# A two-layer graph network on one core: inner Strassen products a step apart, and p1 copied into p2's bank

## The chip, the cores and the metric

The kernel runs on one core of a Trainium2 chip. Its time is device time in microseconds (us) of one execution of the whole program, here the median of three. TensorE (PE) multiplies into PSUM[...]; VectorE (DVE) and ScalarE (ACT) read and write PSUM and SBUF; GpSimd (POOL) works on SBUF only; SyncE (SP) issues the DMAs.

## What is computed

The input x has 16 batches of 1024 nodes with 512 features; adj is one 1024 x 1024 matrix. All values are float32.

```python
# layer 0
h = maximum(layernorm(x), 0)
x = x + (adj @ h[b]) @ weight + bias
# layer 1
u = maximum(layernorm(x), 0)
g = u @ W
s1, s2 = g @ a[:512], g @ a[512:]
e = leaky_relu(s1[:, None] + s2[None, :], 0.2) * adj
x = x + elu(softmax(e, axis=1) @ g + beta * g)
```

## The kernel before

**Products.** Each large product is a 2 x 2 block product by Winograd's form of Strassen: seven products p1 to p7 in place of eight (`PRODUCTS`, line 44). A product takes a left block or block sum (A11, A12, A22, S1 to S4) and a right one (B11, B21, B22, T1 to T4) and adds into one of three pairs of PSUM banks, Y, W or X. Y holds p1, then p1+p6, then +p7, then +p4; X holds p5, then +p3; W holds p2 alone. T1 = B12 - B11, T2 = B22 - T1, T3 = B22 - B12 and T4 = B21 - T2. After each half of a product (`p` or `q`, 0 and 1), `ReadA` (line 121) takes the bank out: ACT copies p1, p6, p5 and p4 to SBUF, DVE adds p2, p7 and p3 to what is there and forms the sums that the next product needs.

**Two layers, two parts each.** A batch of a layer has a first part (layer 0: adj times h, names `y_`; layer 1: the softmax's transpose times u, names `z_`) and a second (times the weights, class `Weighted`, line 322, names `po_` and `pq_`). All 16 batches of layer 0 run first, then all of layer 1.

**The inner level of layer 0.** From batch 1 on, six of the seven products of the first part (all but p7) are themselves seven-product forms on half-size blocks (`inner_steps`, line 206). An inner product has steps in the order r1, r4, r5, r6, r2, r7, r3, two matmuls of 256 columns each (on PE four instructions, 0.86 us). r1 writes a bank of its own, y; ACT copies it out; r5 writes x, which ACT copies out, then r6 and r7 add to y. Step r5's left operand is the first of the sums that `inner_left` (line 405) makes on DVE. After r7 DVE adds the inner sums into the first half of the product's bank, after r3 into the second half. Products run in pairs with their steps alternating: (p1, p2), then (p5, p6), seven turns each; then p3's steps beside p7's plain matmuls; then p4's beside the first product of the second part (lines 279 to 320). Before, p7's first matmul follows p3's first step.

**The order of everything else.** Every engine's instructions stay in the order in which they are written (`InOrder`, line 103). A plan, a dictionary from step number to calls, says what runs after which step: `after(k)`, where k counts the 14 product halves of a part, or in layer 0's inner form 28 turns. The plan of layer 0 (`plan_out`, line 1081) puts beside the products the statistics (`stats`, on ACT), normalisation (`relu`, on ACT, after three small POOL instructions) and logits (`logits`, on DVE) of the batch before, and `inner_left` for p5, p6, p3 and p4 at steps 0, 1, 13 and 18.

**The softmax of layer 1.** While batch b is multiplied, the softmax of batch b+1 is made (`SOFTMAX_A`, line 1144, and `SOFTMAX_B`). `M0` to `M7` make the masked logits of eight chunks (ACT, then DVE with a mask from DRAM), `L2` to `L7` load masks on SP, `X` and `x` send the maxima through DRAM, `N` and `n` read them on DVE, `E0` to `E7` are the exponentials on ACT, each followed at once by its two 32 x 32 transposes on DVE (`exp`, line 795); `S`, `s`, `D` and `d` handle the sums. `LATE_A` (line 1150) forms T3 and T4 of the batch that is being multiplied, in halves a and b: T4a after step 9, T4b after step 11.

**The second part of layer 1** (`layer1_b`, line 867). Of its products p1, p6 and p5 are copied by ACT to SBUF (`part`), p2, p7 and p3 are added to that by DVE (`rest`), and then `elu` takes the result through two activations on ACT and two additions; p4 goes to `elu` straight from PSUM.

The few lines that set the order of layer 1's first part:

```python
    SOFTMAX_A = {
        -1: "M0 L2", 0: "M1 L3", 1: "M2 L4", 2: "M3 L5 X", 3: "M4 L6", 4: "M5 L7", 5: "N B E0",
        6: "M6", 7: "E1 M7 x", 8: "E2", 9: "E3 S", 10: "n b E4", 11: "E5", 12: "E6", 13: "E7 s",
    }
    LATE_A = {5: "T3a", 6: "T3b", 9: "T4a", 11: "T4b"}
```

## Time and profile before

| | |
|---|---|
| median of three runs | 2464.78 us (2459.21 to 2466.63) |
| profiled execution | 2472.3 us, its span 2470.5 us |
| layer 0, from the first product to layer 1's first | up to 1169.15 us |
| a batch of layer 0, as batch 4 | 305.60 to 377.24 us |
| a batch of layer 1, as batch 1 | 1248.85 to 1329.48 us |
| DVE, ACT, POOL busy | 1909.7, 1542.7, 546.2 us |

Most instructions are recorded through helpers and so stand on one line (L111); they are told apart by the names of their tiles: `y_` and `po_` for layer 0, `z_` and `pq_` for layer 1, then the bank (`z_Y`), SBUF blocks (`z_C`, `z_S`), `pT` for the transposed exponentials and their sums T, `in_p` for inner sums, `e` for logits. In a timeline a line has the start, the time, the engine, the operation, out<-in, the number of instructions merged, and in brackets the idle time before it with what ended it. A waits line has the engine and tile that waited, what it waited for, the total in us, the number of times and the longest. A line of stretches has each engine's busy time and instructions, then the granted share of PE's clock, the DMA share and GB/s.

### The profile page before, as it was taken

Reading aid. Unit: us, or ns where it says so; the run is one execution under the profiler, and the core shown is the slowest. Engines: PE = TensorE matmul, PEld = TensorE weight load, DVE = VectorE, ACT = ScalarE, POOL = GpSimd, SP = SyncE. Lnnn points to the kernel's source line nnn. Section 1 sums busy time; section 2 is a strip of 40 time slices with the busy share of each in tenths; the row PEclk is TensorE's granted clock in tenths of the full one; section 3 lists DMA queues with packets and bytes.
Section 4 is the critical chain, followed back from the end, with each engine's and each line's share of the span. In section 5 each row is a group of like instructions: output and inputs, shape, how many; then the busy total and the mean of one; then the engine's idle time right before and its main releaser. Section 6 shows DMA issues by size and latency. Waiting matters only on the chain.

```text
span 2470.5 us, 29533 instructions
## 1 busy us (share of the span) xinstructions
PE 2324.3 (94%) x8344; PEld 1604.4 (65%) x8344; DVE 1909.7 (77%) x4165; ACT 1542.7 (62%) x4115; POOL 546.2 (22%) x680
## 2 busy tenths in 40 slices
PE   9999999999999999999999898988998899999998
PEld 5787777788777777886446544654465546554555
DVE  7777778878877878778787778777877778777864
ACT  3766666676666767664566656665676567556643
POOL 1333221323323222221022202220222012211220
PEclk9999999999999999999999999999999999999999
DMA  6433434433343343325443454445443443344431
GB/s 200 137 128 129 137 121 138 154 120 128 129 145 120 129 154 129 115 99 186 154 147 122 138 165 151 131 131 169 159 128 126 161 155 123 106 141 155 146 97 34
DMA packets 194292, 336.02 MB, mean 136 GB/s; under 512 B 78800, under 2 KB 86992, under 8 KB 194128
## 3 DMA queue, kind: packets, MB, share of 16 engines
q1 hardware_dynamic: 193808, 333.61, 40.9%
q8 instruction: 66, 1.08, 0.2%
q14 instruction: 98, 0.80, 0.1%
q10 hardware_dynamic: 320, 0.52, 0.1%
HBM read 228.33 MB, written 109.91 MB: 137 GB/s over the span
## 4 chain that ended last, share of the span: by engine, by line
PE 27%; DVE 12%; ACT 7%; DMA 5%; SPq 2%; issue 2%; POOL 1%; DVEq 0%; ACTq 0%; POOLq 0%
PE z_Y L111 9%; PE pq_Y L111 8%; ACT e L111 4%; DVE e L111 3%; PE pq_X L111 3%; DMA md<-mx 2%; PE pq_W L111 2%; PE z_X L111 2%; DVE pT L111 2%; PE z_W L111 2%; SPq L111 2%; DVE z_C L111 2%; DMA mask<-maskd 1%; DVE z_S L111 1%; DVE pT_T L111 1%
## 5 line engine op out<-in xcount | busy, mean ns | idle before, releaser
L111 POOL TENSOR_TENSOR x<-x,r 128x512 f32<-128x512 f32 x120 | 209.9, 1762 | 984.9 <-DVE x L111 592.3
L111 ACT ACTIVATE e<-e,nm 128x256 f32<-128x256 f32 x480 | 237.2, 498 | 121.8 <-DVE nm L111 121.8
L111 DVE CUSTOM_DVE_ANT_0 e<-e,mask 128x256 f32<-128x256 f32 x512 | 244.0, 530 | 33.6 <-DMA mask<-maskd 18.1
L111 PE MATMUL z_Y<-pT_T,ul_U 128*128 128x512 f32 x256 | 153.5, 755 | 94.3 <-DVE pT_T L111 94.3
L111 DVE STREAM_TRANSPOSE pT<-e 128x512 f32<-128x512 f32 x240 | 156.3, 689 | 108.3 <-ACT e L111 108.2
L111 PE MATMUL z_Y<-pT,ul_U 128*128 128x512 f32 x512 | 225.2, 592 | 0.0
L111 ACT ACTIVATE e<-s2b,s1b 128x256 f32<-128x256 f32 x512 | 215.0, 504 | 8.7 <-PE po_Y L111 8.7
L111 ACT COPY z_C<-z_Y 128x512 f32<-128x512 f32 x96 | 56.2, 586 | 254.2 <-PE z_Y L111 245.7
L111 POOL TENSOR_TENSOR xr<-xr,bias_bc 128x512 f32<-128x512 f32 x128 | 161.9, 1287 | 222.4 <-DVE xr L111 190.0
L111 PE MATMUL y_Y<-adjT_B,h 128*128 128x512 f32 (+1 forms) x332 | 166.3, 607 | 38.6 <-ACT y_C L111 36.7
L111 PE MATMUL po_Y<-w_c,y_C 128*128 128x256 f32 x768 | 188.3, 379 | 0.0
L111 PEld LDWEIGHTS z_Y<-pT_T,ul_U 128*128 128x128 f32 x256 | 61.5, 248 | 183.6 <-DVE pT_T L111 107.5
L111 DVE CUSTOM_DVE_ANT_0 junk<-xr,v_bc 128x512 f32<-128x512 f32 x240 | 166.4, 693 | 11.1
L111 PE MATMUL pq_Y<-w_c,z_C 128*128 128x256 f32 x768 | 173.7, 379 | 0.0
L111 PEld LDWEIGHTS z_Y<-pT,ul_U 128*128 128x128 f32 x512 | 97.0, 190 | 116.2 <-issue 107.9
L111 PEld LDWEIGHTS pq_Y<-w_c,z_C 128*128 128x128 f32 x768 | 145.8, 190 | 27.1 <-issue 7.7
L111 PEld LDWEIGHTS po_Y<-w_c,y_C 128*128 128x128 f32 x768 | 145.9, 190 | 20.3 <-issue 0.5
L111 ACT ACTIVATE r<-z,rs 128x256 f32<-128x256 f32 x192 | 95.8, 499 | 81.1 <-DVE z L111 81.1
L111 ACT ACTIVATE h<-x,nb_h,r_h 128x512 f32<-128x512 f32 (+1 forms) x132 | 98.2, 793 | 50.2 <-POOL nb_h L111 50.2
L111 ACT ACTIVATE junk<-xr 128x512 f32<-128x512 f32 x120 | 75.9, 632 | 72.6 <-DVE xr L111 70.0
L111 PE MATMUL po_X<-w_c,y_S 128*128 128x256 f32 x512 | 115.7, 379 | 0.0
L111 PE MATMUL pq_X<-w_c,z_S 128*128 128x256 f32 x512 | 115.6, 379 | 0.0
(224 smaller groups left out, 5229.4 us busy)
## 6 DMA issues: line engine op xcount, KB each, us to landing
mask<-maskd SPq DMA_DIRECT2D x128, 512.0 KB
x<-in_x_dram SPq DMA_DIRECT2D x64, 512.0 KB
xr<-in_x_dram SPq DMA_DIRECT2D x256, 128.0 KB
x1d<-xr SPq DMA_DIRECT2D x64, 512.0 KB
ul_U<-ud_U SPq DMA_DIRECT2D x64, 512.0 KB
x<-x1d SPq DMA_DIRECT2D x64, 512.0 KB
out_dram<-x SPq DMA_DIRECT2D x252, 128.0 KB
ud_U<-xr SPq DMA_DIRECT2D x60, 512.0 KB
```

The costliest lines, as they stand in the source:

```text
L111: return lambda *args, **kwargs: tc.keep_in_program_order(f(*args, **kwargs))
```

## The change

In layer 0's inner form the second pair is (p6, p5), and within both pairs the two products are one step apart: the first product's first two steps, then one step of each in turn, then the second's last two. p6's halves are read out after turns 4 and 5, p5's after turn 6. Steps r4 and r5 change places in products that add to a bank already in use (p6, p3, p4). p3's first two steps come before p7's first two matmuls. `inner_left` for p6 and p5 change places; that for p3 stays at step 13.

In layer 1, both parts, ACT copies p1 into p2's bank W, p2 is added to it there without the start flag, and the result is copied out once (first part) or goes straight to `elu` (second part); the second part runs p5 before p2, except in the last batch. The transposes become steps `V0` to `V7` of their own, mostly one step after their exponentials; `M0` moves from step -1 to step 0, and T4b from step 11 to step 10.

```diff
-NODES_LAST = tuple(PRODUCTS[k] for k in (0, 1, 2, 3, 5, 4, 6))
+FORKED = tuple((*p[:4], p[4] and p[0] != "p2", p[5]) for p in PRODUCTS)
+NODES_LAST = tuple(FORKED[k] for k in (0, 1, 2, 3, 5, 4, 6))
+P5_EARLY = tuple(FORKED[k] for k in (0, 3, 1, 2, 4, 5, 6))
...
             if prod == "p1":
+                act.copy(self.fork(p) if self.fork else self.block("C11", p), ps)
+            elif prod == "p2" and self.fork:
                 act.copy(self.block("C11", p), ps)
...
+        def fork(p):
+            banks["W", p] = bank(f"{name}_W{p}")
+            return banks["W", p]
...
-            return [partial(step, r) for r in ("r1", "r4", "r5", "r6", "r2", "r7", "r3")]
+            order = ("r1", "r4", "r5") if first else ("r1", "r5", "r4")
+            return [partial(step, r) for r in (*order, "r6", "r2", "r7", "r3")]
...
-        for pair in (("p1", "p2"), ("p5", "p6")):
-            turns = list(zip(*(inner_steps(prod) for prod in pair)))
-            for m, turn in enumerate(turns):
-                for step in turn:
-                    step()
+        for one, two in (("p1", "p2"), ("p6", "p5")):
+            ones, twos = inner_steps(one), inner_steps(two)
+            turns = ones[0:2] + [t for m in range(5) for t in (twos[m], ones[m + 2])] + twos[5:]
+            for m in range(7):
+                turns[2 * m]()
+                turns[2 * m + 1]()
                 if m == 0 and k:
                     reads("p2", 0)
                     reads("p2", 1)
-                elif m > 4:
-                    for prod in pair:
-                        if prod != "p2":
-                            reads(prod, m - 5)
+                elif m in (4, 5):
+                    reads(one, m - 4)
+                elif m == 6 and k:
+                    reads(two, 0)
+                    reads(two, 1)
                 after(k + m)
...
-        for m in range(7):
-            inn[m]()
-            pla[m if m < 4 else m + 1]()
+        turns = [(inn[0], inn[1]), pla[0:2], (inn[2], pla[2]), (inn[3], pla[3]), (inn[4], pla[4])]
+        turns += [(inn[5], pla[5]), (inn[6], *pla[6:8])]
...
+        def fork(self, kind, q, ps):
+            b = self.banks[kind, q] = bank(f"{self.name}_{kind}{q}")
+            act.copy(b.rearrange("p (i o) -> p i o", i=2), ps)
...
             if prod == "p1":
-                part(0, 0, q, ps)
-            elif prod == "p2":
-                rest(0, 0, q, ps, 2 + q)
+                weighted1[0].fork("W", q, ps)
...
-                elu(1, 0, q, ps, 12 + q)
+                elu(0 if prod == "p2" else 1, 0, q, ps, at[prod] + q)
...
-            (0, inner_left, b, "p5"), (1, inner_left, b, "p6"),
+            (0, inner_left, b, "p6"), (1, inner_left, b, "p5"),
...
     SOFTMAX_A = {
-        -1: "M0 L2", 0: "M1 L3", 1: "M2 L4", 2: "M3 L5 X", 3: "M4 L6", 4: "M5 L7", 5: "N B E0",
-        6: "M6", 7: "E1 M7 x", 8: "E2", 9: "E3 S", 10: "n b E4", 11: "E5", 12: "E6", 13: "E7 s",
+        0: "M0 L2 M1 L3", 1: "M2 L4", 2: "M3 L5 X", 3: "M4 L6", 4: "M5 L7", 5: "N B E0",
+        6: "M6 E1 V0", 7: "M7 x V1", 8: "E2", 9: "E3 V2 S", 10: "n b V3 E4", 11: "E5 V4",
+        12: "E6 V5", 13: "E7 V6 V7 s",
     }
-    LATE_A = {5: "T3a", 6: "T3b", 9: "T4a", 11: "T4b"}
+    LATE_A = {5: "T3a", 6: "T3b", 9: "T4a", 10: "T4b"}
```

## The prediction

> **What bounds the kernel now.** I read the busy shares first, then who waits for whom, then TensorE's timeline in one batch of each layer, and last the queues that end the two waits found there.

> ```profile
> PE 2324.3 (94%) x8344; PEld 1604.4 (65%) x8344; DVE 1909.7 (77%) x4165; ACT 1542.7 (62%) x4115; POOL 546.2 (22%) x680
> ```

> TensorE is the bound, and what can be won is its idle time. Of the waits, two lines are PE's and repeat once in each batch:

> ```profile
> PE z_Y L111 <- DVE pT_T L111: 94.3, 16, 7.6
> ...
> PE y_Y L111 <- ACT y_C L111: 36.7, 15, 3.4
> ```

> PE's timeline in layer 1 (batch 1) shows the first: p4 does its first two chunks, then waits for the second half of T4.

> ```profile
> 1283.19 7.03 PE L111 MATMUL z_X<-pT,ul_S 128*128 128x512 f32 x16
> 1290.05 1.88 PE L111 MATMUL z_Y<-pT_T,ul_U 128*128 128x512 f32 x4
> 1297.28 8.19 PE L111 MATMUL z_Y<-pT_T,ul_U 128*128 128x512 f32 x12 [5.35 <-DVE pT_T L111]
> 1305.31 3.62 PE L111 MATMUL pq_Y<-w_c,z_C 128*128 128x256 f32 x16
> ```

> Sixteen instructions take 6.86 us (1283.19 to 1290.05), so twelve should take 5.15; after the wait they take 8.03. The wait costs more than its length. In layer 0 (batch 4) the same happens at p7's first step:

> ```profile
> 329.77 1.03 PE L111 MATMUL y_p3y<-adjT_B,hS 128*128 128x256 f32 x4
> 333.18 1.79 PE L111 MATMUL y_Y<-adjT_B,h 128*128 128x512 f32 x2 [2.38 <-ACT y_C L111]
> 334.76 1.91 PE L111 MATMUL y_X<-ext,hS 128*128 128x256 f32 x4
> ```

> The stretches behind these waits show why (PEclk is the number after POOL's):

> ```profile
> 333.51:336.92 3.41, 3.41 (x7) 2.03 (x6) 3.31 (x10) 3.33 (x10) 0.00 (x0) 0.50 0.95 219
> ...
> 1297.30:1302.89 5.59, 5.59 (x7) 2.49 (x8) 1.84 (x3) 1.74 (x6) 0.00 (x0) 0.50 0.71 269
> ```

> [...] half clock for 3.41 us in layer 0 and up to 6.8 in layer 1. [...] 2.38 us were enough, while 1.92 us in one window were not (layer 1, batch 0: idle from 1212.23, half clock only from 1217.56, so the window before the wholly idle one ended at 1214.15). [...] For the copy's price I use this trace's row (586 ns from PSUM to SBUF)[...].

> **What the waits are worth.** Layer 1: one batch is 112 instructions of 429 ns and 112 of 216 ns, 72.2 us; sixteen are 1155.5. PE's first there starts at 1169.15 and its last ends at 2460.9: 1291.7. So 136 us are lost, about 8.5 a batch. Layer 0: from p3's first step (329.77) to p4's (347.02) are 17.25 us, for seven steps of 0.864 and eight of 0.858, 12.91: 4.34 us lost a batch in 14 batches, 61 in all. The last batch has three waits (1.72, 3.39, 0.63) and loses 8.2. Everything else on PE is dense.

> **Layer 1, T4 and the transposes.** DVE's timeline before that wait:

> ```profile
> 1286.82 0.69 DVE L111 TENSOR_TENSOR z_C<-z_X,z_C 128x512 f32<-128x512 f32 x1
> ...
> 1289.84 0.17 DVE L111 TENSOR_SCALAR nm<-nm 128x16 f32<-128x16 f32 x1
> 1292.16 1.30 DVE L111 STREAM_TRANSPOSE pT<-e 128x512 f32<-128x512 f32 x2 [2.14 <-ACT e L111]
> 1293.39 0.65 DVE L111 TENSOR_TENSOR z_C<-z_X,z_C 128x512 f32<-128x512 f32 x1
> ...
> 1296.01 1.22 DVE L111 TENSOR_TENSOR pT_T<-pT,pT_T 128x1024 f32<-128x1024 f32 x1
> ```

> T4's second half stands at step 11, behind the 0.47 us maximum, a wait of 2.14 for ACT's exponentials, their transposes (1.23) and p3's second read (2.62). At step 10 it follows the first read directly: 1286.82 + 2.73 + 1.22 is 1290.8. PE needs it at 1290.05 + 1.72 = 1291.8, so the wait goes, with 1.0 us to spare. Ahead of that read, the work on DVE is the same: two pairs of transposes behind mask 7 before (E2, E3), two after (V1, V2). The waits for ACT's exponentials fall away there, but masks 6 and 7 still come from DMA at their own time. So DVE's lateness at that read stays. Read in every batch against PE's end, it is 0.0 to 0.9 us in twelve, and 1.3 to 2.2 in batches 2, 4, 8 and 9. Beyond 1.0 it becomes a wait of PE: about 0.9, 0.6, 1.2 and 0.3, 3 us together, too short for the half clock. What moves behind: the maximum and exponentials 4 to 7 start 1.2 us later, so ACT's copies of p4 and of pq's p1 slip to 1 or 2 us after PE; pq's p5, now second, gives 3.45 us cover before p2 needs them. Cover gone would cost about 1 us a batch. The moved mask steps 0 and 1 issue two loads (512 KB each) on SP later by one step; SP then waits for the maxima of step 2 as before.

> **Layer 1, p1 copied into p2's bank.** Removed: four DVE additions a batch (z_C with z_W, z with pq_W), 4 x 0.60 = 2.4 us of DVE, and ACT's copies of p1 change only their target; two ACT copies out of W come (0.48 each). New wait: PE's p2 follows ACT's copy of p1. ACT is busy with the last batch's ELU until 3.3 to 4.5 us after a batch's start; copy, masks 0 and 1 (8 x 0.40), second copy: done by 8.8. PE needs it at 10.3. Bound: nothing, to 1 us a batch if ACT is 2.5 us later than that; I take nothing. In layer 1's second part p6 now stands right before p7 in the same bank: copy due in 1.7 us, taking 0.6.

> Sum for layer 1: 136 minus 3, a gain of **132**.

> **Layer 0, the order of the inner steps.** ACT's queue before p7:

> ```profile
> 328.94 1.52 ACT L111 ACTIVATE xr<-xr,nb_u,r_u 128x512 f32<-128x512 f32 x2 [1.74 <-POOL nb_u L111]
> 330.37 0.35 ACT L111 COPY y_p5t<-y_p5y 128x256 f32<-128x256 f32 x1
> ...
> 332.54 0.59 ACT L111 COPY y_C<-y_Y 128x512 f32<-128x512 f32 x1 [0.47 <-DVE y_Y L111]
> ```

> p6's last copies stand behind a normalisation that waits for POOL. In the new order p6's r7 is step 10 of 14 instead of 12, ahead of that normalisation, and p7 begins two p3 steps later instead of one. Counted through from 326.7, where ACT ends the statistics of that step: copy 0.37, DVE addition 0.70, copy out to 328.4. p7 could start at 331.5, so **its wait goes**. But what is late next? p3's r5 is now its second step, at 330.65, and its left operand is the first sum of inner_left p3, which stays at step 13, behind p5's last additions on DVE. The chain: normalisation 328.45 to 329.9 (POOL's 1.6 us end at 328.4), copy of p6's second half to 330.4 (its addition follows a 1.46 us logit step on DVE), p5's r7 copy to 330.76, two DVE additions (0.60 each) to 331.98, the sum 0.42: 332.4. PE waits **1.8 us**. It cannot be under 0.3: p5's r3 ends at 317.69 + 12.09 = 329.78[...], and one addition and the sum follow, 1.02 and some 0.1 of signalling, 330.9 to 331.1. Upwards, 0.5 of ACT or POOL lateness makes it 2.4, and then the half clock (another 1.7). I take 1.8 without it, since 1.92 in a window did not trigger. So 4.34 becomes 1.8: 14 x 2.54 = 36; in the last batch I take 8.2 to 5: 3. Gain **39**. The banks are no new wait: p5's inner bank can be p1's, freed some 4 us before. The r5 step of p4 has sums that were ready 6 us before.

> **Sum.** 132 + 39 = 171. The profiled execution took 2472.3 (span 2470.5); 171 less is 2301. The median of the runs stands 0.3% below it at 2464.78, so 6.9% less is **2294**.

> **Rivals.** A: r5's sum comes in time but for a least wait of 0.4. For it: ACT would only have to be 1.4 us ahead. Against: POOL's step sits in the chain. 14 x 1.4 = 20 less: 2274. B: that wait exceeds 2 us and takes the half clock too: 14 x (0.4 + 1.7) = 30 more: 2324. C: DVE (1910 - 38 us of work in 2300) is late by 2.5 us in every layer 1 batch because less PE idle leaves it less time to catch up: 16 x 1.5 = 24 more, 2318; with the half clock added in part, 2345. D, the slower side: mask 7's load. Its wait in DVE's queue stands ahead of both halves of T4. SP's chain (maxima out and back, 4 us, then stores, then loads) does not shrink with the batch. If the masks land so late that DVE is 10 us late at p3's read, PE waits 8.9 and runs slow for 2.6: 16 x 11.5 = 184, against 136 now, and with layer 0's gain the time is 2475. It decides from about 9.3 us of lateness; the most seen is 2.2. E: the moves leave T4's wait as it is (the queue is pinned to the written order, so I see no way): 2464.8 - 39 = 2426.

> **Chances.** Forecast 0.52 (its own range 2280 to 2310), A 0.13, B 0.16, C 0.14, D 0.02, E 0.03. The range from 2266 to 2335 leaves out D, E and the ends of C and A. 0.3%, 7 us, is about what can be told from no change here; faster 0.97, same 0.01, slower 0.02.

> **What would show it.** Right: no PE wait for pT_T over 2 us, none of y_Y for y_C, batches of about 72.3 and 69.1 us, and a new wait of PE y_p3x for DVE in_p near 1.8. Wrong: PE waits at z_W for ACT's copy, clock 0.50 in layer 0, or a DVE in layer 1 that meets each p3 read late.

## The result, and the profile after

The changed kernel takes **2329.24 us** (median of four runs, 2327.41 to 2333.91), the kernel before 2464.66 (2459.21 to 2466.63): ratio 0.9457, interval 0.9436 to 0.9478. The forecast was 2294, the range 2266 to 2335. The profiled execution took 2327.41 us, its span 2325.6.

The busy shares come first, as before. PE's own busy time fell by 47.6 us although it has the same 8344 instructions, since fewer of them ran at half clock (granted clock 0.990 over the span, 0.967 before); DVE's fell by 44.6.

```profile
PE 2276.7 (98%) x8344; PEld 1587.3 (68%) x8344; DVE 1865.1 (80%) x4101; ACT 1544.3 (66%) x4147; POOL 529.3 (23%) x680
```

Then who waits for whom, PE's lines:

```profile
PE y_p3x L115 <- DVE in_p L115: 28.4, 15, 2.0
PE y_p5y L115 <- DVE y_p5t L115: 4.6, 1, 4.6
PE z_Y L115 <- DVE pT_T L115: 1.9, 2, 1.1
```

The wait for T4 (`pT_T`) has fallen from 94.3 us to 1.9. The wait of p7 for ACT (`y_Y` for `y_C`, 36.7) is gone, and the foreseen wait of p3's r5 for the first sum of `inner_left` stands in its place, 2.0 us in each of batches 1 to 14.

Layer 1 first, PE's timeline in the second batch of the layer, and below it DVE's:

```profile
1263.53 5.74 PE L115 MATMUL z_X<-pT,ul_S 128*128 128x512 f32 x13
1269.11 7.03 PE L115 MATMUL z_Y<-pT_T,ul_U 128*128 128x512 f32 x16
```

```profile
1265.88 0.69 DVE L115 TENSOR_TENSOR z_C<-z_X,z_C 128x512 f32<-128x512 f32 x1 [0.39 <-PE z_X L115]
...
1268.61 1.22 DVE L115 TENSOR_TENSOR pT_T<-pT,pT_T 128x1024 f32<-128x1024 f32 x1
1269.74 0.25 DVE L115 TENSOR_REDUCE nm<-mall 128x16 f32<-128x64 f32 x1
```

p4's sixteen matmuls now run as one piece. T4's second half follows p3's first read directly and ends at 1269.83, before the second maximum. p4's third chunk is due at 1269.11 + 4 x 0.429 = 1270.83, so the spare time is 1.0 us, as the prediction had it.

Layer 0, PE in batch 4, and the stretches around the wait (PEclk is the number after POOL's):

```profile
324.28 1.03 PE L115 MATMUL y_p3y<-adjT_B,hS 128*128 128x256 f32 x4
327.32 1.15 PE L115 MATMUL y_p3x<-ext,in_p 128*128 128x256 f32 x4 [2.02 <-DVE in_p L115]
328.27 3.57 PE L115 MATMUL y_Y<-adjT_B,h 128*128 128x512 f32 x4
331.68 1.03 PE L115 MATMUL y_X<-ext,hS 128*128 128x256 f32 x4
```

```profile
324.75:328.17 3.42, 1.40 (x7) 0.95 (x6) 2.58 (x6) 2.22 (x5) 0.00 (x0) 1.00 0.75 244
328.17:331.58 3.41, 3.41 (x6) 1.40 (x5) 2.85 (x9) 2.94 (x10) 0.00 (x0) 0.51 1.00 214
```

After the wait p7's four 512-wide matmuls take 3.41 us from start to start where four take 1.72: the half clock is back (granted clock 0.51 in the stretch from 328.17, 1.00 in the one with the wait). These stretches are windows of 3.41 us, the steps in which the granted clock changes in the trace. In batch 1 the same wait, of the same length (2.02 us), lies across the border of two windows:

```profile
113.20:116.61 3.41, 1.75 (x9) 1.20 (x7) 2.48 (x6) 2.63 (x6) 0.00 (x0) 1.00 0.45 153
116.61:120.03 3.42, 3.06 (x10) 2.01 (x11) 3.31 (x10) 2.64 (x8) 0.00 (x0) 1.00 0.92 242
```

There the clock stays at 1.00. So PE loses 3.94 us in the first case and 2.25 in the second.

In what follows, PE's **loss** is what its instructions take from start to start beyond their usual 429 ns (512 columns) or 216 ns (256 columns), summed over a place. Before and after:

| loss of PE, us | before | forecast | after |
|---|---|---|---|
| layer 0, batches 1 to 14 | 61 (14 x 4.34) | 25 (14 x 1.8) | 46.7 (9 x 3.94, 5 x 2.25) |
| layer 0, last batch | 8.2 | 5 | 9.6 |
| layer 1 | 136 | 3 | 4.2 |

The differences add to 145 us, which is what the two profiled executions differ by (2472.3 - 2327.4).

### The profile page after: what moved, and what is told of

It reads as the page before. It is cut to its first block, busy times and chain, and to the rows that moved or that the text cites. A ratio compares the mean times of both kernels' runs of the same rounds, so it can differ in the third digit from the quotient of the medians.

```text
span 2325.6 us, 29418 instructions
## 1 busy us (share of the span) xinstructions
PE 2276.7 (98%) x8344; PEld 1587.3 (68%) x8344; DVE 1865.1 (80%) x4101; ACT 1544.3 (66%) x4147; POOL 529.3 (23%) x680
## 4 chain that ended last, share of the span: by engine, by line
PE 81%; ACT 7%; DVE 7%; DMA 3%; issue 2%; SPq 1%; POOL 0%; DVEq 0%; ACTq 0%; POOLq 0%
PE z_Y L115 15%; PE y_Y L115 10%; PE po_Y L115 10%; PE pq_Y L115 8%; PE z_X L115 7%; PE po_X L115 5%; PE pq_X L115 4%; PE z_W L115 4%; PE y_W L115 3%; ACT xr L115 2%; PE po_W L115 2%; PE y_X L115 2%; PE pq_W L115 2%; ACT junk L115 2%; PE y_p1y L115 2%; PE y_p4y L115 2%
## 5 line engine op out<-in xcount | busy, mean ns | idle before, releaser
L115 POOL TENSOR_TENSOR x<-x,r 128x512 f32<-128x512 f32 x120 | 198.9, 1674 | 883.7 <-DVE x L115 325.3
L115 DVE CUSTOM_DVE_ANT_0 e<-e,mask 128x256 f32<-128x256 f32 x512 | 226.4, 498 | 105.8 <-DMA mask<-maskd 88.3
L115 PE MATMUL y_Y<-adjT_B,h 128*128 128x512 f32 (+1 forms) x332 | 160.1, 596 | 1.6 <-ACT adjT_B L115 1.6
L115 PE MATMUL z_Y<-pT_T,ul_U 128*128 128x512 f32 x256 | 113.3, 594 | 2.1 <-DVE pT_T L115 1.9
L115 PE MATMUL z_W<-pT,ul_U 128*128 128x512 f32 x256 | 112.5, 592 | 0.0
L115 PE MATMUL z_Y<-pT_T,ul_S 128*128 128x512 f32 x256 | 112.5, 592 | 0.0
L115 PE MATMUL z_X<-pT_T,ul_S 128*128 128x512 f32 x256 | 112.5, 592 | 0.0
```

The costliest lines, as they stand in the source:

```text
L115: return lambda *args, **kwargs: tc.keep_in_program_order(f(*args, **kwargs))
```

## The experiments

The theory was: layer 1's gain is T4's place in DVE's queue; what layer 0 still loses is the place of p3's sums, and the half clock behind that wait comes from 2 us of idle in one window. The rivals: the other parts of layer 1's change carry part of the gain; the lateness in layer 0 only moves on when its cause is moved; the half clock comes from any wait there. The kernel before took 2467.5, 2467.7 and 2464.8 us beside the three groups of runs.

**The two layers apart.** The first kernel is the one before with the edits of layer 1 only, the second with those of layer 0 only (the hunks that the section on the change describes for each).

> The kernel before with only the changes of layer 1 (p1 copied into p2's bank, T4's second half at step 10, transposes in steps of their own). If the gain of layer 1 is the removed wait for T4, its loss of 135 us falls to about 4 as in the changed kernel, and layer 0 keeps its 69 us: about 2465 - 131 = 2334 us. If the two layers' changes help each other, it would be well above that, 2345 or more.

> The kernel before with only the changes of layer 0 (pairs one step apart, p6 before p5, r5 second in p6, p3 and p4). By the trace of the changed kernel layer 0 loses 56 us instead of 69, so about 2465 - 13 = 2452 us, with 14 waits of y_p3x for in_p near 2 us and layer 1 as before (wait of z_Y for pT_T near 94 us in all). If layer 0's changes were worth the 39 us forecast and layer 1 gave less, it would be 2426.

Layer 1 alone: 2339.48 us, ratio 0.9484 (0.9471 to 0.9497). Layer 0 alone: 2456.1, ratio 0.9956 (0.9943 to 0.9970). Taken off 2464.7 these are 127 and 11 us, together 138 for the 135 measured: the layers do not help or hinder each other beyond a few us. Layer 0's edits are worth 11 us (7 to 14 by the interval), not the 39 of the forecast.

**T4's step alone.** One number of the kernel before:

```diff
-    LATE_A = {5: "T3a", 6: "T3b", 9: "T4a", 11: "T4b"}
+    LATE_A = {5: "T3a", 6: "T3b", 9: "T4a", 10: "T4b"}
```

> The kernel before with one number changed: T4's second half stands at step 10 in place of 11; exponentials with their transposes, p1's additions and layer 0 stay. If the wait for T4 is only a matter of that place in DVE's queue, its end comes at 1290.8 for a need at 1291.8 in batch 1 as in the changed kernel and nearly all of the 131 us is gained: 2334 to 2345 us. If the transposes' new steps and the four saved additions are needed to bring DVE in time, a wait of some 2 to 3 us stays in most batches and, with the half clock, 16 x 3 to 16 x 5 of the 131 come back: 2382 to 2414.

2335.77 us, ratio 0.9473 (0.9460 to 0.9486). The two longest of PE's waits in this kernel:

```profile
PE y_Y L111 <- ACT y_C L111: 36.8, 15, 3.4
PE y_p5y L111 <- DVE y_p5t L111: 1.8, 1, 1.8
```

No line for `pT_T` is left; layer 0's wait is untouched. One digit gives all of layer 1's gain. p1's copy, the transposes' own steps and the moved masks are not needed for it.

**T4's step put back.** The changed kernel with the same digit undone (10 to 11).

> The changed kernel with T4's second half put back from step 10 to step 11; all else stays changed. There it stands on DVE behind the second maximum (0.47 us), one pair of transposes (1.3) and p3's second read (2.6): in a batch that starts like the third of layer 1, it would end 4.4 us after PE needs it. If the place in DVE's queue is the cause, PE waits some 4.4 us in each of 16 batches and takes half clock behind it, 6 to 6.5 in all: 2329 + 100 = 2429 us, 2410 to 2440. If the new steps of the transposes and p1's copy into p2's bank were what removed the wait, hardly anything comes back: under 2350.

2420.23 us, ratio 0.9812 (0.9781 to 0.9843): 91 us of the gain go, against 100 expected. PE's wait is back (here in the profiled execution, which at 2412.26 was the fastest of the four):

```profile
PE z_Y L115 <- DVE pT_T L115: 61.9, 16, 5.2
```

It is 61.9 us, not 94.3, and layer 1 loses 89 us instead of 136. The kernel with layer 0's edits alone, which differs from this one in the other edits of layer 1, takes 2456.1 us, some 35 more. So these edits do shorten the path to T4 when T4 stands behind the transposes. They are a second way to part of the same gain, and buy nothing once T4 stands ahead. Which of them shortens it was not tested.

**T4's step and the copy into p2's bank.** The kernel before with T4's digit and the edits for `FORKED`, `fork` and `P5_EARLY`.

> The kernel before with T4's second half at step 10 and p1 copied into p2's bank (and p5 early in the second part); exponentials with their transposes and the masks' steps as before, layer 0 as before. With T4's move alone DVE is nowhere late in layer 1, so the 38 us of additions that go from DVE buy nothing: 2336 us, within 3. If the copy into the bank is what makes the layer 1 changes together 3.7 us slower than T4's move alone, 2340. If it shortens the path after all, 2332 or less.

2337.81 us, ratio 0.9473 (0.9459 to 0.9488), beside 0.9473 without the copy: no difference. PE never waits at `z_W`. The 2 us up to layer 1's full set (0.9484) lie within the intervals, so no cost of the transposes' steps is shown.

**p3's sums one step earlier.** The changed kernel with

```diff
-            (13, inner_left, b, "p3"), (15, o.logits, 1, 1, 0), (16, o.logits, 1, 1, 1),
+            (12, inner_left, b, "p3"), (15, o.logits, 1, 1, 0), (16, o.logits, 1, 1, 1),
```

> The changed kernel with one number changed: the sums of p3's inner product (inner_left p3) stand at step 12 in place of 13, on DVE ahead of p5's last additions. If the 2.0 us wait of y_p3x for in_p and the half clock behind it are all that layer 0 loses, they go together (14 waits, 46.7 us): 2329 - 46 = 2283 us, and no half clock in batches 1 to 14. If the lateness only moves on, since p5's read-out is then 1.4 us later on DVE, p3's r4 or p7's later steps wait for y_X or y_C instead: 0.5 to 2 us a batch, 2290 to 2311. If the wait shrinks below 1.9 us without going, the half clock alone goes: 2329 - 15 = 2314.

2298.56 us, ratio 0.9322 (0.9309 to 0.9335): 31 us faster than the changed kernel, not 46. The wait for `in_p` is gone and no batch from 1 to 14 has half clock (the granted clock over the span is 0.996, 0.990 in the changed kernel), but another wait came:

```profile
PE y_p3y L115 <- DVE y_p3t L115: 14.2, 15, 1.0
```

DVE's timeline in batch 4 of this kernel shows what it stands behind, POOL's why:

```profile
326.57 0.08 DVE L115 DVE_READ_ACCUMULATOR2_ANT s<- 128x1 f32 x1
329.84 0.17 DVE L115 COPY s2t<-s 128x8 f32<-128x8 f32 x1 [3.19 <-POOL s2t L115]
330.05 0.21 DVE L115 STREAM_TRANSPOSE s2t<-s2t 128x32 f32<-128x32 f32 x1
330.19 0.38 DVE L115 TENSOR_TENSOR y_p3t<-y_p3y,in_p 128x256 f32<-128x256 f32 x1
```

```profile
328.51 0.19 POOL L115 TENSOR_SCALAR r_h<-mv_h 128x2 f32<-128x2 f32 x1 [9.39 <-ACT h L115]
...
329.69 0.12 POOL L115 MEMSET s2t<- 128x32 f32 x1
```

The logits' store (step 16) copies into a tile that POOL clears first; the memset is queued behind a normalisation that waits 9.4 us for ACT's statistics. DVE idles 3.2 us in front of the addition of p3's r6, which PE needs before r7 writes the same bank. DVE's wait lay in the changed kernel too, but there PE was 2 to 4 us later and did not meet it:

```profile
333.70 0.17 DVE L115 COPY s2t<-s 128x8 f32<-128x8 f32 x1 [2.58 <-POOL s2t L115]
```

**The logits' store behind that addition.** On top of the edit before:

```diff
-            (16, o.store_logits), (18, inner_left, b, "p4"),
+            (17, o.store_logits), (18, inner_left, b, "p4"),
```

> The changed kernel with the sums of p3 at step 12 and the logits' store (a DVE copy that waits for a POOL memset queued behind POOL's normalisation steps) at step 17 in place of 16, so behind the addition of p3's r6 on DVE. With the sums at step 12 alone, PE waits 0.98 us (1.25 lost) in 14 batches for that addition, which stands behind the copy's wait of 3.2 us. If that is the whole of the new wait, 14 x 1.25 = 17 us go: 2298.6 - 17 = 2281. If the wait only moves on to p7's read-out or p4's sums behind the copy, 0.3 to 1 us a batch stays: 2286 to 2299.

2279.6 us, ratio 0.9241 (0.9227 to 0.9254): 19 us less. In layer 0's batches 1 to 14 PE loses nothing more; 8.2 us in the last batch and 3.6 in layer 1 stay.

**The half clock.** The sums of p3 between p5's two additions, so that the wait shrinks but stays:

```diff
                 turns[2 * m]()
+                if m == 6 and k:
+                    after(k + m - 0.5)
                 turns[2 * m + 1]()
...
-            (13, inner_left, b, "p3"),
+            (12.5, inner_left, b, "p3"),
```

> The changed kernel with p3's sums put between p5's two last additions on DVE instead of behind both: the first sum comes 0.6 us earlier, the second addition 1.4 us later. PE's wait of y_p3x for in_p should fall from 2.02 to 1.42 us. If 2 us of idle in one clock window is what brings the half clock, no batch has it any more: 14 x (1.42 + 0.25) = 23 us lost instead of 46.7, so 2329 - 23 = 2306 us. If the half clock comes from any wait there, however short, 9 batches still take it and only 14 x 0.6 = 8 us go: 2321. A further 14 x 1 us may be lost to the wait for the addition of p3's r6, if the later read-out moves that as it did with the sums at step 12: then 2319.

2311.43 us, ratio 0.9374 (0.9360 to 0.9388). PE's two longest waits are now

```profile
PE y_p3x L115 <- DVE in_p L115: 20.3, 15, 1.4
PE y_p3y L115 <- DVE y_p3t L115: 6.1, 15, 0.9
```

The first is 1.42 us a time as expected and costs 1.66; no batch from 1 to 14 has half clock (granted clock 0.998 over the span). The second, behind the logits' store, is 0.37 us in those batches (0.64 lost). Batches 1 to 14 lose 14 x 2.30 = 32 us, against 46.7 in the changed kernel. Without half clock the changed kernel would have lost 14 x 2.25 = 31.5. So the two waits together are as long as the one was, and the gain, 15 us by the traces and 18 by the medians, is the clock's. That any wait there brings it is ruled out: this one of 1.42 us did not.

**r5 third again.** The changed kernel with

```diff
-            order = ("r1", "r4", "r5") if first else ("r1", "r5", "r4")
+            order = ("r1", "r4", "r5")
```

> The changed kernel with r5 third again in p6, p3 and p4 (r1, r4, r5). p3's second step is then r4, which adds into the bank that holds p5; ACT's copy of p5's first half out of that bank ends at 326.88 in the batch whose r5 now waits until 327.3 and could start at 325.2. If the step order only chooses which late producer PE meets, PE waits 1.7 us for that copy, y_X for ACT y_C, under the 2 us that bring the half clock: 14 x 2.0 = 28 us lost in place of 46.7, about 2310 us. If r5 second is needed for layer 0's gain, since p6 or p4 now meet a late copy too, 2329 or more.

2308.7 us, ratio 0.9362 (0.9345 to 0.9379): 21 us **faster** than the changed kernel. PE now meets the other late producer:

```profile
PE y_X L115 <- ACT y_C L115: 23.8, 15, 1.7
```

1.67 us a time, 1.94 lost, and no half clock in batches 1 to 14 (granted clock 0.997 over the span). p7's old wait for `y_C` does not return. So r5 as second step is not what removed it, but the rest of layer 0's edits: the pairs one step apart, p6 ahead of p5, and p3's two first steps ahead of p7. No run tells these apart. r5 as the second step by itself cost 0.35 us of wait and, in nine batches, the clock.

**The last batch of layer 0.** On top of the two edits, in `FIRST_A`:

```diff
-        1: "R0", 4: "R1", 7: "B E0 V0 R2", 10: "E1 V1 R3", 12: "R4", 15: "E2 V2", 18: "b R5",
+        1: "R0", 4: "R1", 7: "B E0 V0 R2", 10: "R3", 12: "R4", 15: "E1", 16: "E2 V1", 18: "V2 b R5",
```

> As the changed kernel with p3's sums at step 12 and the logits' store at step 17, and in layer 0's last batch the second exponentials and their transposes moved from step 10 to steps 15 and 16, the third's transposes to 18. In the last batch PE now loses 8 to 9.6 us, nearly all behind DVE's wait of 3 us for these exponentials. If only their place is at fault, 7 to 8 us go on top of the two other edits: 2273 us. If their later release of the buffers delays other tiles, or the softmax of layer 1's first batch becomes late, the gain stays within 3 us or turns into a loss: 2278 to 2285.

2278.18 us, ratio 0.9232 (0.9217 to 0.9248), against 0.9241: not told apart. The 4.7 us wait for `y_p5t` fell to 0.4, as expected, but p3's r5 then waits for `in_p`, and the loss there went from 8.2 to 6.4 only.

```profile
PE y_p3x L115 <- DVE in_p L115: 2.7, 1, 2.7
```

What delays the sums in that batch was not followed further.

**The short list of edits.** The kernel before with layer 0's changes, T4's digit, the sums at step 12 and the store at step 17, but none of layer 1's other changes.

> The kernel before with the changes of layer 0, T4's second half at step 10, p3's sums at step 12 and the logits' store at step 17, but without the rest of layer 1's changes: p1 is added by DVE as before, the transposes follow their exponentials at once, the masks keep their steps. It differs from the changed kernel with the two edits of layer 0 (2279.6 us) in those alone. If they buy nothing, as on top of the kernel before, 2276 to 2280. If their 38 us less of DVE work matter now that PE waits hardly anywhere, it is slower: 2285 to 2295.

2278.11 us, ratio 0.9239 (0.9225 to 0.9253), against 0.9241 with all of layer 1's changes. The work that these take from DVE (busy 1897.4 us here, 1862.9 with them) is not on the path here either. This kernel and the two before it that have both edits are not told apart, and are the fastest found. No run has the edits of the two steps without layer 0's reordering.

## Why the prediction was right, and where it was not

**Layer 1, right in size and cause.** 136 us were to fall to 3; they fell to 4.2. The named step, T4 ahead of the exponentials and their transposes, is shown by one digit set alone (2335.77) and undone alone (2420.23). The residual waits were foreseen as 0.9, 0.6, 1.2 and 0.3 us in batches 2, 4, 8 and 9. They came as two for `pT_T`, 0.8 in batch 2 and 1.1 in batch 9, with less than 0.2 in batch 6 and 0.4 for an ACT tile of the second part (`z`) in batch 4. That the total fits so well is therefore in part chance. The price of nothing for p1's copy held: no wait at `z_W`, and no difference in time. Rivals C, D and E did not come, since no wait for T4 is over 1.1 us.

**Layer 0, p7's wait: right.** It is gone, and the next late thing is the one named, p3's r5 on `in_p` from DVE. Two terms of the sum were mis-sized:

- *"I take 1.8 without it"*, the half clock. The working counted from the moment when p3's r1 is done at PE's pace; there it had ACT's copy of p5's r7 end at +0.11 us, the sum at +1.75, and PE start with it. In batch 4 of the trace that moment is 324.28 + 0.86 = 325.14. Lines of ACT and DVE:

```profile
322.72 0.58 ACT L115 COPY y_C<-y_Y 128x512 f32<-128x512 f32 x1 [1.23 <-DVE y_Y L115]
323.20 1.52 ACT L115 ACTIVATE xr<-xr,nb_u,r_u 128x512 f32<-128x512 f32 x2
...
325.15 0.38 ACT L115 COPY y_p5t<-y_p5y 128x256 f32<-128x256 f32 x1
```

```profile
325.56 1.29 DVE L115 TENSOR_TENSOR y_X<-y_X,y_p5t 128x512 f32<-128x512 f32 x2 [0.93 <-ACT y_p5t L115]
326.76 0.41 DVE L115 TENSOR_TENSOR in_p<-hS 128x256 f32<-128x256 f32 x1
```

  The copy ends at 325.53 (+0.39), the sum at 327.17 (+2.03), and PE starts at 327.32 (+2.18). So 0.28 us came in ACT's queue, and 0.15 lie between the sum's end and PE's start, which the working had left out. The normalisation does not wait for POOL there, as I thought, but follows ACT's copy of p6, which waits for DVE's `y_Y`. DVE's queue shows the step that the working skipped: between ACT's copy of p6's r7 and the addition into `y_Y`, which it put at one addition of 0.70 us, DVE first forms the inner sum `y_p6t`.

```profile
321.53 0.43 DVE L115 TENSOR_TENSOR y_p6t<-y_p6y,in_p 128x256 f32<-128x256 f32 x1 [0.27 <-ACT y_p6t L115]
321.99 0.70 DVE L115 TENSOR_TENSOR y_Y<-y_Y,y_p6t 128x512 f32<-128x512 f32 x1
```

  That puts the addition 0.46 us later; the other items of the chain came 0.18 us shorter, and 0.28 remain. With the 0.07 us by which PE's first instruction runs longer, 1.8 became 2.25. Without the clock this error costs 14 x 0.45 = 6 us; with it nine batches lose 1.69 more (3.94 against 2.25), another 15. The gain per batch was to be 2.54; it was 0.4 in nine and 2.1 in five. This is rival B ("that wait exceeds 2 us and takes the half clock too"), in nine batches of 14. The prediction had named the danger, though its sum there was off: 0.5 us of lateness on 1.75 makes 2.25, not 2.4. The 0.28 and the 0.15 were enough.
- *"in the last batch I take 8.2 to 5"*. It became 9.6. That figure had no working behind it. DVE waits 2.97 us there for the second exponentials of layer 1's first softmax, with the inner sums of p5 and p6 behind it, and PE 4.65:

```profile
1105.46 1.30 DVE L115 STREAM_TRANSPOSE pT<-er 128x512 f32<-128x512 f32 x2 [2.97 <-ACT er L115]
```

```profile
1107.13 2.08 PE L115 MATMUL y_p5y<-adjT_T,hS 128*128 128x256 f32 x4 [4.65 <-DVE y_p5t L115]
```

  The run that moved these exponentials shows it, and also that the place is then late in p3.

Together: layer 0 gains 13 us in place of 39, 26 short. The other 9 of the 35 us come from carrying 6.9% over to the median: the profiled execution stands 7.6 us above its median before and 1.8 below it after. No cause for that scatter was sought. The measured 2329 lies in the stated range, but outside the forecast's own 2280 to 2310 and nearest to the 2324 of rival B, which had a chance of 0.16. The range held because it was drawn wide enough to take B in. That B's number itself comes so near is in part chance: B has the half clock in all 14 batches where nine have it, and the step to the median makes up for that.

**What it did not see.** That the logits' store would be the next wait once p3's sums come in time, and that r5 as second step was itself the dearer order (2329 against 2309). Rival A, the sum in time, was priced at a least wait of 0.4 us for the sum behind p5's additions; with the sum moved ahead of them that wait is nothing, but the store then takes 1.25.

## What to carry to other kernels

Ask of each edit in a bundle what it gives alone: here one digit in a schedule gave some 130 of 135 us, and two more such digits, on top of layer 0's reordering, another 50, while the structural part of layer 1 gave nothing that could be measured once that digit was set. When a wait goes, look at every engine's queue for what the late engine has been hiding: a wait of DVE for a POOL memset cost nothing until PE came 2 us earlier. And where a remaining wait is near the size that was followed by half clock (here 2.02 us was in nine batches of 14, 1.67 in none), an estimate of it to 0.4 us is not good enough: price both sides, and give the dearer one its weight by where the wait falls on the grid of the granted clock.

## What the runs showed of the hardware

PE's idle time can be counted in each window of that grid after the first 60 us of these two traces: from the end of an instruction's 0.216 or 0.429 us to the next start, windows that are at half clock themselves left out. The least that was followed by half clock was 2.12 us (after, 963.12 to 966.54), the most that was not was 2.18 (before, 1371.16 to 1374.58). The 1.92 us of the prediction, taken from the recorded end of an instruction, are 2.08 by this count.

So the same wait of 2.02 us cost 3.94 us in the nine batches of the kernel after where one window held 2.12 to 2.25 us of the idle time, and 2.25 us in the five where a border divided it and the larger part was 1.70 to 1.83. The wait of 1.67 us with r5 third again, 1.84 of idle in the batch from 321.62, had no half clock behind it.
